# Restormer block, float32, one core: weight set-up behind the first LayerNorm, two more bands of depthwise convolution on TensorE, and a new issue order

## The chip, the cores and the metric

The kernel runs on one core of one Trainium2 chip. A core has five engines with a queue of instructions each: TensorE (PE: matmuls and transposes into PSUM), VectorE (DVE), ScalarE (ACT), GpSimd (POOL) and SyncE (SP); 16 DMA engines move data between the core's memory (SBUF) and HBM, or within SBUF. An engine takes its instructions in the order in which the program issued them, and waits on semaphores for the others. The metric is the device time of one execution in microseconds, the median of several runs. Everything is float32.

## What is computed

One transformer block on x of shape (16, 128, 96, 96): channel attention, then a feed-forward network with a depthwise 3x3 convolution. Cut to what matters:

```python
B, C, H, W = (16, 128, 96, 96); HEADS = 8; HID = 4 * C
x_hwc = x.transpose(0, 2, 3, 1)
xn1 = _layernorm(x_hwc, ln1_w, ln1_b)                  # LN1, over the 128 channels of each pixel
# attention over channels: q, k, v = xn1 @ w.T, q and k normalised over all 9216 pixels of an image,
# 16x16 attention per head, then @ wp.T
x = x + attn_out.transpose(0, 3, 1, 2)
xn2 = _layernorm(x_hwc, ln2_w, ln2_b).transpose(0, 3, 1, 2)   # LN2
h1 = jnp.einsum('bchw,oc->bohw', xn2, w_in[:, :, 0, 0])       # 128 -> 512 channels
h2 = lax.conv_general_dilated(h1, w_dw, ..., feature_group_count=HID)   # depthwise 3x3
h3 = jax.nn.gelu(h2, approximate=False)
x = x + jnp.einsum('bchw,oc->bohw', h3, w_out[:, :, 0, 0])    # 512 -> 128 channels
```

The kernel never forms q, k and v: it accumulates the Gram matrix of LN1's output over an image on TensorE, works out attention as one 128x128 matrix from it, and applies that matrix to the normalised pixels. So an image's attention can be worked out only when LN1 of the whole image is done.

## The kernel before

An image is cut into 8 bands of 12 rows (128 bands in all, numbered g), a band into 3 units of 4 rows, the 512 hidden channels into 4 chunks of 128. For a chunk of a band the depthwise convolution is done in one of two ways. In the usual way TensorE makes the hidden rows (`hidden`), ScalarE copies them out of PSUM (`kept`) and makes three or four of the nine products with a tap's weight, GpSimd issues DMAs that add two or three of these up and into the sum, VectorE does the other taps, and ScalarE applies gelu. For chunk 3 of some bands, TensorE does the convolution itself: nine matmuls of a unit with `comp`, the product of the tap's weight and w_in, accumulate in one PSUM bank; there is no hidden tensor, and gelu reads PSUM. `by_pe` says which bands:

```python
PE_CHUNK = 3
PE_BANDS = (0, 2, 4, 6, 8, 10)
PE_OF = 11
...
    def by_pe(g):
        return (NG - 1 - g) % PE_OF in PE_BANDS
    ...
        jobs += [(g, n) for n in range(NCH) if n != PE_CHUNK or not by_pe(g)]
```

The usual way, cut:

```python
    last = j == len(jobs) - 1
    third = n == THIRD_CHUNK and g % THIRD_OF in THIRD
    dma_taps = () if last else DMA_TAPS[: 3 if third else 2]
    left = [t for t in range(1, 9) if t not in dma_taps]
    for k, (r, e) in enumerate(chunks):                 # three pieces of a band's rows
        pe(..., at("hidden", jk), lambda r=r, e=e: hidden(r, e), ...)
        act(..., at("kept", jk), lambda r=r, e=e: kept(r, e), ...)
    act(..., at("product", j), lambda: product(0), h1, h3)
    for k, t in enumerate(dma_taps):
        act(..., at("products", jk), lambda t=t: product(t), h1, [("pr", (jn, t))])
    for k, t in enumerate(dma_taps[1:]):
        add(at("add_last", j), lambda t=t: add_products(t), ...)      # DMA, accumulating
    for k, t in enumerate(left):
        dve(..., at("tap", j + STEP["tap"] * k), lambda t=t: tap(t), h1, h3, True)
    if dma_taps:
        add(at("add_first", j), lambda: add_products(DMA_TAPS[0]), [pr[0]], h3)
    ...
        act(..., at("gelu", j), lambda s=s, e=e: gelu(s, e), [], h3[s:e])
```

The order in which instructions are issued is worked out on the host, before the launch, by a small plan. Every operation is entered with its engine, an assumed duration, what it reads and writes, a place (`at(kind, place)`: a position in the sequence of jobs plus a number per kind from the table `AT`), and the time after which its result is assumed to be there. The plan steps through time: an idle engine takes, of the operations whose inputs it takes to be ready and which find a buffer, the one with the lowest place. The order so found is the program; the chip keeps it, whatever the real times are.

```python
    def at(kind, place):
        return place + AT[kind]
```

The set-up of the weights is entered first. One operation on ScalarE's queue issues five weight loads; then TensorE transposes wq, wk and wp, then w_in, w_out and the nine tap products, four blocks to a PSUM bank, and VectorE copies each bank out:

```python
    op("ACT", 400, at("load_a", p), loads, [], mine, 900 + SLACK, dma=2 * T_MOVE)
    dve(400, at("weights", p), shifts, [], [("w", "in"), ("w", "conv"), ("w", "shift")])
    transposed(lambda: [v["wqk"][:, :P], v["wqk"][:, P:], v["wp"]], keep_qkp, ["qk"])
    ...
    transposed(lambda: [v["win"][:, n, :] for n in range(NCH)], ..., ["in"])       # winT
    transposed(lambda: [v["wout"][:, n * P : (n + 1) * P] for n in range(NCH)], ..., ["out"])
    for t0 in (0, 4, 8):                                                            # comp
        ...
```

LN1 and LN2 take 18 batches of four tiles of 128 pixels an image: TensorE transposes them (`forth`), VectorE takes statistics (BATCH_NORM_STATS2), GpSimd does the power -1/2, ScalarE (and for image 0 VectorE too) scales them into `zT`, TensorE adds zT to the Gram matrix (LN1) and transposes back (`back`), and ScalarE copies the result out (`place`).

Of the kernel before, what the change touches and what calls it, by code (L numbers as in the profile page):

```python
# [19 lines left out]
PE_CHUNK = 3  # L20
PE_BANDS = (0, 2, 4, 6, 8, 10)
PE_OF = 11
TINY = 1e-20
DMA_TAPS = (1, 2, 3)
THIRD, THIRD_OF, THIRD_CHUNK = (0,), 2, 1
# [3 lines left out]
X1_BUFS, XB_BUFS, PR_BUFS, H3_BUFS, ZT_BUFS = 2, 6, 5, 10, 3  # L29
IN_TURN = ("tr", "h3", "pr", "xb", "x1")  # L30
AT = dict(
    weights=13.95, zeros=3.15, load_a=-16.5, forth_a=-13.65, stats_a=-3.7, variance_a=-8.5, power_a=2.25,
    shift_a=-7.7, scaled_a=-1.8, gram=-2.7, back_a=-20.15, place_a=-18.95, attention=-16.9, mix=-10.45,
    residual=-13.95, mixed=-8.95, add_x=12.85, forth_b=-11.4, stats_b=-5.65, variance_b=-8.6,
    power_b=-18.6, shift_b=-25.05, scaled_b=-1.65, back_b=-21.6, place_b=-2.25, halo=2.3, hidden=-0.85,
    kept=-5.15, product=-7.7, products=3.3, add_last=-8.75, tap=4.45, add_first=25.8, gelu=-10.75,
    conv=0.1, conv_gelu=-5.7, out=3.25, add=-0.45, store=1.1,
)
STEP = dict(scaled=0.3, hidden=0.1, products=0.5, tap=0.166, conv=1.6, conv_tap=0.03, out=0.8, out_part=0.05)
SLACK = 300  # L40
NORM1_END = 6.0
EARLY = 5
WAIT = dict(POOL=350, SP=1300, ACT=1300)
T_POWER = 1000
T_ADD, T_MOVE = 3100, 1800


class Plan:
# [14 lines left out]
    def op(self, engine, ns, place, work, reads, writes, result, own=None, dma=0, two=False):  # L63

        k = len(self.ops)
        needs = {}  # L70
        for t in reads:
            if t in self.writer:
                needs[self.writer[t]] = True
        for t in writes:
            if t in self.writer:
                needs[self.writer[t]] = True
            for r in self.readers.get(t, ()):
                needs[r] = True
        for t in reads:
            self.readers.setdefault(t, []).append(k)  # L80
        new = []
        for t in writes:
            self.writer[t], self.readers[t] = k, []
            if t[0] in self.free and t[:2] not in self.users and t[:2] not in new:
                new.append(t[:2])
        for t in {t[:2]: None for t in (*reads, *writes)}:
            if t[0] in self.free:
                self.users.setdefault(t, []).append(k)
                needs[self.users[t][0]] = True
        needs.pop(k, None)  # L90
        self.ops.append((engine, ns, place, work, list(needs), new, result, own or result, dma, two))

    def order(self):
# [38 lines left out]
        def dispatch(engine, time):  # L132
# [19 lines left out]
            if o[8]:  # L152
                self.dma = max(time + ns + WAIT[engine], self.dma) + o[8]
                result = own = self.dma + result - time
# [48 lines left out]
def tile_restormer_block(  # L203
# [28 lines left out]
    NB, NU, UPB = H // BR, H // UR, BR // UR  # L232
# [101 lines left out]
    op = plan.op  # L334

    def at(kind, place):
        return place + AT[kind]

    def bank(key, n=4 * P):

        return banks[plan.slot["h", key]][:, :n]
# [18 lines left out]
    def pe(ns, p, f, r, w):  # L360
        op("PE", ns, p, f, r, w, ns + 200 + SLACK, ns)

    def dve(ns, p, f, r, w, two=False):
        op("DVE", ns, p, f, r, w, ns + 120 + SLACK, ns + 120, two=two)
# [29 lines left out]
    def weights(p):  # L394

        mine = [("h3", ("weights", k)) for k in range(2)]
        v, names = staged, iter(range(99))

        def loads():
            a, b = (h3p.tile([P, BR * W], F32, tag="h3", name=f"weights_{k}") for k in range(2))  # L400
            v["win"] = a[:, :HID].rearrange("p (n c) -> p n c", c=P)
            v["wout"], v["wp"] = a[:, HID : 2 * HID], a[:, 2 * HID : 2 * HID + P]
            v["wqk"], v["wqkT"] = b[:, : 2 * P], b[:, 2 * P : 4 * P]
            v["wt"] = b[:, 4 * P : 8 * P].rearrange("p (t c) -> p t c", c=P)
            nc.scalar.dma_start(out=v["wqk"][:, :P], in_=wq)
            nc.scalar.dma_start(out=v["wqk"][:, P:], in_=wk)
            nc.scalar.dma_start(out=v["wp"], in_=wp)
            nc.scalar.dma_start(out=v["win"], in_=w_in.rearrange("(n p) c kh kw -> p n (c kh kw)", p=P))
            nc.scalar.dma_start(out=v["wout"], in_=w_out.rearrange("c j kh kw -> c (j kh kw)"))

        def transposed(parts, kept, gives):

            key = ("weights", next(names))
            h = ("h", key)
            d = {}

            def forth():
                d["pt"] = bank(key)
                for k, part in enumerate(parts()):
                    nc.tensor.transpose(d["pt"][:, k * P : (k + 1) * P], part, ident)  # L420

            pe(440, at("weights", p), forth, mine, [h])
            dve(700, at("weights", p), lambda: kept(d["pt"]), [h], [("w", g) for g in gives] + mine[1:])

        def keep_qkp(pt):
            nc.vector.tensor_copy(v["wqkT"], pt[:, : 2 * P])
            nc.vector.tensor_scalar(wqkT, pt[:, : 2 * P], w1, None, ALU.mult)
            nc.vector.tensor_copy(wpT, pt[:, 2 * P : 3 * P])

        def biases():  # L430
            v["pc"] = bank(("weights", "biases"))[:1, : 2 * P]
            nc.tensor.matmul(v["pc"], lhsT=b1, rhs=v["wqkT"], start=True, stop=True)

        def comp_parts(ts):
            for t in ts:
                nc.vector.tensor_scalar(
                    v["wt"][:, t % 4, :], v["win"][:, PE_CHUNK, :], dw[:, PE_CHUNK, t : t + 1], None, ALU.mult
                )

        def shifts():  # L440

            nc.vector.tensor_tensor(none, w2, w2, ALU.mult)
            nc.vector.tensor_scalar(none, none, TINY * TINY, TINY, ALU.is_lt, ALU.mult)
            nc.vector.tensor_add(w2, w2, none)
            nc.vector.reciprocal(none, w2)
            nc.vector.tensor_mul(b2, b2, none)

        op("ACT", 400, at("load_a", p), loads, [], mine, 900 + SLACK, dma=2 * T_MOVE)
        dve(400, at("weights", p), shifts, [], [("w", "in"), ("w", "conv"), ("w", "shift")])
        transposed(  # L450
            lambda: [v["wqk"][:, :P], v["wqk"][:, P:], v["wp"]], keep_qkp, ["qk"]
        )
        pe(440, at("weights", p), biases, [("w", "qk"), mine[1]], [("h", ("weights", "biases"))])
        dve(400, at("weights", p), lambda: nc.vector.tensor_copy(cqk, v["pc"]), [("h", ("weights", "biases"))], [("w", "qk")])
        transposed(
            lambda: [v["win"][:, n, :] for n in range(NCH)],
            lambda pt: nc.vector.tensor_scalar(winT.rearrange("p n c -> p (n c)"), pt, w2, None, ALU.mult), ["in"],
        )
        transposed(
            lambda: [v["wout"][:, n * P : (n + 1) * P] for n in range(NCH)],  # L460
            lambda pt: nc.vector.tensor_copy(woutT.rearrange("p n c -> p (n c)"), pt), ["out"],
        )
        for t0 in (0, 4, 8):
            ts = range(t0, min(t0 + 4, 9))
            dve(170 * len(ts), at("weights", p), lambda ts=ts: comp_parts(ts), [mine[0]], [mine[1]])
            transposed(
                lambda ts=ts: [v["wt"][:, t % 4, :] for t in ts],
                lambda pt, ts=ts: nc.vector.tensor_scalar(
                    comp[:, ts[0] : ts[-1] + 1, :].rearrange("p t c -> p (t c)"), pt[:, : len(ts) * P],
                    w2, None, ALU.mult,  # L470
                ), ["conv"],
            )
# [18 lines left out]
    def norm(i, second, place_of):  # L491
# [41 lines left out]
        def pixels(s, m):  # L533
# [75 lines left out]
            dve(80, at("variance" + ab, s), variance, [], [bt])  # L609
            op("POOL", T_POWER, at("power" + ab, s), power, [], [bt], T_POWER + 33 + SLACK)  # L610
            dve(80, at("shift" + ab, s), shift, [], [bt])
# [320 lines left out]
            move(at("store", p), lambda: store(0, UPB), [("xb", (i, b), k) for k in range(UPB)], [], T_MOVE)  # L932

    def by_pe(g):
        return (NG - 1 - g) % PE_OF in PE_BANDS

    NG = B * NB
    jobs, first = [], []
    for g in range(NG):
        first.append(len(jobs))  # L940
        jobs += [(g, n) for n in range(NCH) if n != PE_CHUNK or not by_pe(g)]
# [3 lines left out]
    def job_of(g):  # L945

        return g * band

    weights(-17.0)
    zeros(-17.0)  # L950
    for i in range(B):
# [44 lines left out]
```

## Time and profile before

| | before |
|---|---|
| time, median of 3 runs | 4349.23 us (4347.39 to 4353.22) |
| span of the profiled execution | 4350.3 us |
| VectorE: taps of the convolution (L838) | 2590 x 1408 ns |
| TensorE: convolution matmuls (L889) | 3780 records, two to a float32 matmul |
| ScalarE: products (L834) | 946 x 1389 ns and 442 x 1366 ns |
| first tap on VectorE starts at | 103.02 us |

A profile is one execution of the program. In the table of engines each has its busy time, its share of the span, and the number of its instructions. In a row of stretches of time the same stands for a piece of the span, with the granted clock of TensorE and the share of the DMA engines. In the order of time a row gives the start, the length, the engine, the line of the kernel, the operation, and in brackets how long the engine was idle before it and what released it. A "q" behind an engine's name is its queue issuing a DMA; PEld is TensorE loading weights, which overlaps its matmuls.

### The profile page before, as it was taken

The page shows a single profiled execution, that of the slowest core. Times are in us where ns is not written, and L with a number is a line of the kernel's source. Part 1 is how long each engine was busy: PE and PEld are TensorE (multiplying, and loading weights), DVE is VectorE, ACT ScalarE, POOL GpSimd, SP SyncE. Part 2 cuts the span into 40 slices and gives each one's busy share as a digit, 9 for nine tenths or more (in the row PEclk, how much of TensorE's full clock was granted, in tenths as well). Part 3 has the DMA queues.
Part 4 walks back from the last instruction along what each step waited for, and adds up shares of the span by engine and source line. Part 5 has one row for each costly group of instructions (what it writes and reads, how often), then busy time and mean ns, then how long its engine had stood idle before and what let it go on. Part 6 is the DMA issues. An engine that isn't in the chain of part 4 may idle for free. (4 is left out here: it accounts for less than half of the span.)

```text
span 4350.3 us, 53308 instructions
## 1 busy us (share of the span) xinstructions
PE 4261.9 (98%) x17638; PEld 2717.5 (62%) x17638; DVE 4212.9 (97%) x5638; ACT 4136.9 (95%) x7240; POOL 1964.4 (45%) x1725
## 2 busy tenths in 40 slices
PE   7999999999999999999999999999999999999998
PEld 6666666666666666666666666666666666666554
DVE  6999999999999999999999999999999999999999
ACT  4999999999999999999999999999999999999996
POOL 3444544444444444444445444444444444454331
PEclk9999999999999999999999999999999999999999
DMA  2788898988998889888898988988889898898997
GB/s 79 161 183 190 170 202 179 186 189 174 192 192 186 183 173 193 180 189 180 180 190 188 190 178 176 192 189 181 183 184 191 174 200 178 179 196 160 190 185 156
DMA packets 193572, 785.23 MB, mean 180 GB/s; under 512 B 22416, under 2 KB 23824, under 8 KB 193296
## 3 DMA queue, kind: packets, MB, share of 16 engines
q0 software_dynamic: 153792, 630.00, 76.7%
q1 hardware_dynamic: 37152, 151.01, 9.6%
q8 instruction: 140, 2.29, 0.2%
q10 hardware_dynamic: 2352, 0.81, 0.1%
q14 instruction: 136, 1.11, 0.1%
HBM read 148.26 MB, written 75.50 MB: 51 GB/s over the span
## 5 line engine op out<-in xcount | busy, mean ns | idle before, releaser
L838 DVE SCALAR_TENSOR_TENSOR h<-h,dw,h 128x1152 f32<-128x1152 f32 x2590 | 3588.1, 1408 | 10.1 <-ACT h L834 6.9
L889 PE MATMUL h<-xn,comp 128*128 128x384 f32 x3780 | 1365.1, 486 | 2.2 <-ACT h L823 2.2
L834 ACT ACTIVATE pr<-h,dw 128x1152 f32<-128x1152 f32 x946 | 1290.5, 1389 | 3.9 <-DMA pr<-pr 3.6
L912 PE MATMUL h<-h,woutT 128*128 128x384 f32 x3072 | 1149.2, 489 | 13.2 <-ACT h L823 4.8
L818 PE MATMUL h<-xn,winT 128*128 128x384 f32 (+1 forms) x2652 | 1051.6, 503 | 25.1 <-ACT h L823 14.2
L889 PEld LDWEIGHTS h<-xn,comp 128*128 128x128 f32 x3780 | 689.7, 189 | 431.4 <-issue 9.2
L842 POOL DMA_DIRECT2D pr<-pr x505 | 461.9, 915 | 823.0 <-ACT pr L834 656.5
L823 ACT COPY h<-h 128x384 f32<-128x384 f32 (+1 forms) x1326 | 727.6, 607 | 61.6 <-PE h L818 49.2
L912 PEld LDWEIGHTS h<-h,woutT 128*128 128x128 f32 x3072 | 557.7, 190 | 355.8 <-issue 16.9
L842 POOL DMA_DIRECT2D h<-pr x441 | 425.0, 964 | 701.9 <-PE h L818 98.8
L818 PEld LDWEIGHTS h<-xn,winT 128*128 128x128 f32 x2652 | 472.3, 190 | 331.4 <-issue 47.9
L567 POOL TENSOR_TENSOR rstd_a<-ve_a,mhalf 128x4 f32<-128x4 f32 x288 | 517.3, 1799 | 326.8 <-DVE ve_a L563 311.6
L567 POOL TENSOR_TENSOR rstd_b<-ve_b,mhalf 128x4 f32<-128x4 f32 x288 | 526.9, 1830 | 295.1 <-DVE ve_b L563 276.6
L846 ACT ACTIVATE h<-h 128x1152 f32<-128x1152 f32 (+1 forms) x444 | 561.4, 1265 | 50.6 <-DMA h<-pr 48.5
L834 ACT ACTIVATE h<-h,dw 128x1152 f32<-128x1152 f32 x442 | 603.3, 1366 | 5.4 <-PE h L912 3.3
L588 ACT ACTIVATE zT<-pT_b,nb_b,rstd_b 128x128 f32<-128x128 f32 x1132 | 459.1, 580 | 1.4 <-DVE nb_b L571 0.7
L588 ACT ACTIVATE zT<-pT_a,nb_a,rstd_a 128x128 f32<-128x128 f32 x1080 | 442.9, 601 | 4.0 <-DVE nb_a L571 3.9
L598 PEld LDWEIGHTS g<-zT 128*128 128x128 f32 x2304 | 297.4, 192 | 57.6 <-issue 5.6
L598 PE MATMUL g<-zT 128*128 128x129 f32 x2304 | 305.5, 275 | 0.0
L507 PE MATMUL h<-xn,mwT 128*128 128x384 f32 x768 | 288.0, 488 | 3.1 <-ACT h L823 1.0
L632 ACT ACTIVATE xn<-pB_b,b 128x384 f32<-128x384 f32 x384 | 270.6, 705 | 8.8 <-PE pB_b L628 8.8
L634 ACT COPY xn<-pB_a 128x384 f32<-128x384 f32 x384 | 237.2, 618 | 23.9 <-PE pB_a L628 23.7
(145 smaller groups left out, 3371.4 us busy)
## 6 DMA issues: line engine op xcount, KB each, us to landing
pr<-pr POOLq DMA_DIRECT2D x505, 576.0 KB, 6.1
h<-pr POOLq DMA_DIRECT2D x441, 576.0 KB, 6.8
x<-in_x_dram SPq DMA_DIRECT2D x128, 576.0 KB, 6.4
out_dram<-x SPq DMA_DIRECT2D x127, 576.0 KB, 5.4
x<-in_x_dram POOLq DMA_DIRECT2D x122, 576.0 KB, 7.3
out_dram<-x SPq DMA_DIRECT2D x3, 192.0 KB, 1.9
weights<-in_L_conv_w_in_dram ACTq DMA_DIRECT2D x1, 256.0 KB, 10.8
weights<-in_L_conv_w_out_dram ACTq DMA_DIRECT2D x1, 256.0 KB, 11.7
```

Source lines behind the costliest of these rows:

```text
L507: nc.tensor.matmul(rows(pm), lhsT=mats[i][0], rhs=interior(i, u), start=True, stop=True)
L567: nc.gpsimd.tensor_tensor(rstd, d["ve"], mhalf, ALU.pow)
L588: nc.scalar.activation(zT(q)[:, k, :P], d["pT", q][:, k, :], AF.Identity, bias=d["nb"][:, t : t + 1], scale=d["rstd"][:, t : t + 1],)
L598: nc.tensor.matmul(grams[i][:, : P + 1], lhsT=zt[:, :P], rhs=zt, start=(q == 0 and k == 0), stop=(q == NU * TPU // QT - 1 and k == QT - 1),)
L818: nc.tensor.matmul(rows(ph), lhsT=winT[:, n, :], rhs=window(xn, r0 + r, e - r, 1), start=True, stop=True)
L823: nc.scalar.copy(window(h1_, r, e - r, 1), rows(d.pop(("ph", r))))
L834: nc.scalar.activation(to, shifted(t), AF.Copy, scale=dw[:, n, t : t + 1])
L838: nc.vector.scalar_tensor_tensor(h3, shifted(t), dw[:, n, t : t + 1], h3, ALU.mult, ALU.add)
L842: nc.gpsimd.dma_start(out=to, in_=d["pr", t], accum_op=ALU.add)
L846: nc.scalar.activation(h3, h3, AF.Gelu)
L889: nc.tensor.matmul(d["pc"], lhsT=comp[:, t, :], rhs=window(xn, r0 + dy, UR, dx), start=(t == 0), stop=(t == 8),)
L912: nc.tensor.matmul(rows(d["po"]), lhsT=woutT[:, n, :], rhs=h3s[g, n][:, s * UR : (s + 1) * UR, :], start=(k == 0), stop=(k == NCH - 1),)
```

## The change

Three things are changed, all in the plan that fixes the order. First, the plan takes the weights as loaded only after 20 us instead of 1.2 us beyond their transfer, so that the set-up's transposes are ordered behind LN1's first batches: TensorE is not to stand before a weight that has not landed while image data have. Second, in the last image six of the eight bands have chunk 3 convolved by TensorE, where the old rule gave four: the last image has no LN1 of a next image beside it. Counted from the end these are bands 0, 1, 2, 4, 5 and 7 instead of 0, 2, 4 and 6; all other images keep the old rule. Third, the numbers of the table `AT` are new, so that every queue has a new order. Buffers, instructions and the rest of the arithmetic are the same.

```diff
+PE_LAST = (0, 1, 2, 4, 5, 7)
...
 AT = dict(
-    weights=13.95, zeros=3.15, load_a=-16.5, forth_a=-13.65, stats_a=-3.7, variance_a=-8.5, power_a=2.25,
-    shift_a=-7.7, scaled_a=-1.8, gram=-2.7, back_a=-20.15, place_a=-18.95, attention=-16.9, mix=-10.45,
-    residual=-13.95, mixed=-8.95, add_x=12.85, forth_b=-11.4, stats_b=-5.65, variance_b=-8.6,
-    power_b=-18.6, shift_b=-25.05, scaled_b=-1.65, back_b=-21.6, place_b=-2.25, halo=2.3, hidden=-0.85,
-    kept=-5.15, product=-7.7, products=3.3, add_last=-8.75, tap=4.45, add_first=25.8, gelu=-10.75,
-    conv=0.1, conv_gelu=-5.7, out=3.25, add=-0.45, store=1.1,
+    weights=10.45, zeros=-0.55, load_a=-15.15, forth_a=-12.6, stats_a=-5.05, variance_a=-7.4,
+    power_a=-1.65, shift_a=-5.8, scaled_a=-2.25, gram=-2.15, back_a=-19.55, place_a=-30,
+    attention=-11.35, mix=-10.3, residual=-15.8, mixed=-15.6, add_x=2.25, forth_b=-11.95, stats_b=-3.7,
+    variance_b=-5.4, power_b=-20.6, shift_b=-22.65, scaled_b=-2.4, back_b=-19.15, place_b=-0.55,
+    halo=4.55, hidden=-1.65, kept=-8.9, product=-7.6, products=2.05, add_last=-4.65, tap=7.3,
+    add_first=25.4, gelu=-4.85, conv=-0.8, conv_gelu=-6.2, out=2.3, add=7.1, store=-8.95,
 )
...
+T_WEIGHTS = 20000
...
-        op("ACT", 400, at("load_a", p), loads, [], mine, 900 + SLACK, dma=2 * T_MOVE)
+        op("ACT", 400, at("load_a", p), loads, [], mine, T_WEIGHTS, dma=2 * T_MOVE)
...
     def by_pe(g):
-        return (NG - 1 - g) % PE_OF in PE_BANDS
+        k = NG - 1 - g
+        return k in PE_LAST if k < NB else k % PE_OF in PE_BANDS
```

## Prediction, before the changed kernel was run

> **What bounds the kernel now.** I read the table of engines first, then the middle and the end of the span by stretches of time, and last the opening in order of time. The first says only that four engines are nearly full:
>
> ```profile
> PE 4261.9 (98%) x17638; PEld 2717.5 (62%) x17638; DVE 4212.9 (97%) x5638; ACT 4136.9 (95%) x7240; POOL 1964.4 (45%) x1725
> ```
>
> The stretches show where the few idle microseconds lie (columns: stretch, its length, then busy us and instructions of PE, PEld, DVE, ACT, POOL; granted clock, DMA share, GB/s):
>
> ```profile
> 0.00:25.00 25.00, 9.12 (x34) 6.22 (x35) 7.70 (x30) 3.16 (x6) 6.16 (x26) 0.86 0.66 221
> 25.00:50.00 25.00, 23.61 (x194) 22.66 (x194) 19.96 (x76) 15.54 (x39) 12.71 (x26) 0.94 0.01 2
> 50.00:75.00 25.00, 20.30 (x130) 16.77 (x129) 14.66 (x52) 10.48 (x27) 4.66 (x5) 0.81 0.19 50
> ...
> 1000.00:2000.00 1000.00, 991.10 (x4109) 630.92 (x4108) 974.66 (x1297) 970.92 (x1705) 468.22 (x397) 1.00 0.89 185
> ...
> 4050.00:4250.00 200.00, 190.27 (x653) 111.78 (x652) 198.06 (x217) 188.17 (x303) 76.08 (x71) 0.99 0.93 187
> 4250.00:4300.00 50.00, 42.36 (x121) 23.91 (x120) 48.45 (x41) 38.21 (x51) 11.29 (x13) 0.90 0.77 160
> 4300.00:4351.00 51.00, 40.32 (x118) 22.39 (x116) 44.96 (x39) 20.70 (x28) 6.90 (x8) 0.95 0.66 145
> ```
>
> Three regimes. In the middle VectorE is busy 974.7 of 1000 us, ScalarE 970.9, and TensorE is level with them. TensorE's busy figure counts overlapping matmuls, so I rate it by throughput instead: in the chain of waits, ten records of 384 columns take 3.23 us, so 0.323 us each (a float32 matmul of the program is two records), a 480-column one by scaling 0.404; sixteen 128-column Gram records took 1.95 us, 0.112 each after the first. Between 1000 and 2000 us the groups list 2304 records of 384 columns, 104 of 480 and 1593 of 128, plus some tens of small ones: 744 + 42 + 178 + about 15 = 979 us. So three engines are within 1% of each other and the middle has no single bound. In the last 300 us VectorE alone is full (291.5 of 301 us) and ScalarE and TensorE loosen. In the first 75 us every engine is idle part of the time, so a latency chain rules there:
>
> ```profile
> 8.37 0.45 PE L420 MATMUL h<-ident,weights 128*128 128x128 f32 x1 [8.37 <-DMA weights<-in_L_conv_wq_dram]
> ...
> 11.43 0.48 PE L420 MATMUL h<-ident,weights 128*128 128x128 f32 x1 [1.94 <-DMA weights<-in_L_conv_wp_dram]
> ...
> 11.69 1.92 PE L549 MATMUL h<-ident,x 128*128 128x128 f32 x8
> ...
> 18.54 1.09 PE L420 MATMUL h<-ident,weights 128*128 128x128 f32 x4 [3.99 <-DMA weights<-in_L_conv_w_in_dram]
> 19.67 0.75 DVE L457 TENSOR_SCALAR winT<-h,w 128x512 f32<-128x512 f32 x1 [4.47 <-PE h L420]
> ...
> 20.87 0.71 DVE L580 TENSOR_SCALAR zT<-h,st_a,rstd_a 128x128 f32<-128x128 f32 x2
> ...
> 58.88 0.29 DVE L694 COPY gs<-g 128x129 f32<-128x129 f32 x1 [0.75 <-PE g L598]
> ```
>
> The reader is to see that TensorE waits for three small weights up to 11.43 us and again 3.99 us for w_in, while image data are there already: the first image transpose at 11.69 has no wait of its own. The first normalised tile is made only at 20.87 us; the Gram sum of image 0, which attention needs, is copied at 58.88 us; the first convolution tap of VectorE starts at 103.02 us.
>
> **What the skill says.** PSUM — Partial Sum Buffer, Engine vs sequencer instructions, states that the queues of ScalarE, VectorE and GpSimd are strict FIFO and that matmuls start in program order. The trace agrees: the image's transpose stands still behind a weight's. TensorE: Matmul & The Clock Gate, What's actually happening, says that an idle window of about 3.4 us drops the array to half clock; here, after the 3.99 us wait, the granted clock was 0.50 from 18 to 27 us. Perfetto Trace Analysis, Identifying the Most-Contended Engine, warns that matmul busy time is no measure of TensorE's headroom; hence my throughput count.
>
> **Part 1, setup behind LN1.** Nothing is removed. In the order of the changed kernel TensorE begins with the transposes of x bands 0 and 1, and the first weight transpose stands only after LN1 batch 17's transposes; the weight loads are issued in the same place as before. VectorE still begins with the five small operations on the LN2 weights, which waited for a load until 7.20 us and end at 8.13 us. x band 0 is issued at 0.81 us and the nine x loads took 3.9 us at the least to land, 5.6 in the median, so it is there by about 6.5. So the first statistics come at about 8.2 us where they came at 12.87; then as before some 1.1 us of statistics, 0.15, one power of 1.01 us and 0.15 with their hand-overs, so that the first scaling comes at about 11.5 us instead of 20.87: 9.4 us earlier. From there to the Gram copy took 38.0 us for 18 batches. I keep that: in both orders eight setup matmuls stand inside this stretch (0.15 us each: four took 0.60), and the half-clock stretch only moves. Behind the Gram the new order has 13 setup matmuls where the old had 5, which I put at 1 us. All bands of x had landed by 18.9 us (the DMA share falls to zero), so bands do not run short. Attention and the run-up to the first tap keep their order nearly (182 rows of VectorE before the first tap, 186 before), so the first tap should start at about 94 us (103.02 - 9.4 + 1), 9 us earlier. It lies on the path: behind it all three engines are full. **-9 us.**
>
> **Part 2, two more bands on TensorE.** The old rule took bands 0, 2, 4, 6 from the end; the new takes 0, 1, 2, 4, 5, 7. For each of the two net bands:
> - VectorE loses 6 taps of 1.41 us: 8.5 us. Both: 16.9 us.
> - TensorE gains 27 matmuls, 54 records x 0.323 = 17.4 us, and loses three hidden matmuls, 4 x 0.404 + 2 x 0.323 = 2.3 us. Net 15.2 us. Both: 30.4 us.
> - ScalarE loses 3 products of 1.29, 3 copies (1.7 us together) and a gelu of 1.20, and gains 3 gelus of about 0.55: 5.1 us. Both: 10 us. Two accumulating DMAs a band go too.
>
> From 4050 us on TensorE's throughput time is 730 x 0.323 + 30 x 0.404 + 130 x 0.112 = 262.5 us of 301. It becomes 292.9; VectorE's 291.5 becomes 274.6. So the bound of the tail passes from VectorE at 291.5 to TensorE at 292.9: the two bands overshoot the balance, and an honest sum gives about 0. What speaks for a small gain is the drain: before, TensorE was idle at the end while VectorE finished, and the new order puts all of the last three bands' chunk 3 on TensorE, ahead of the last taps. I choose **-3 us** between -10 and +5.
>
> **Part 3, the new order.** Some 37 priorities change and every queue is reshuffled; the work and the 32 table loads of ScalarE are the same. Idle in the middle is about 2.5% of VectorE, 2% of TensorE: 100 us in all, of which a re-tuning on the same structure might win or lose a tenth. The order was presumably chosen for a lower end, so **-4 us**, between -16 and +12. No row of the profile fixes this; it is the loosest term.
>
> Sum: 4349 - 9 - 3 - 4 = 4333 us.
>
> **Rivals.** (a) The start is hidden: LN1 starts earlier, but attention 0 waits for the weights now transposed behind it, or the first bands wait for winT and comp. For it: wqkT, cqk, winT and comp stand between LN1 batch 17 and the attention steps in the new order, and comp's nine parts pass through VectorE in turn. Against: 13 matmuls, five evacuations of 0.3 to 0.75 us and comp's nine products of 0.27 us are some 8 us spread over two engines that were busy only 14.66 and 20.30 of 25 us between 50 and 75 us. That rival would leave 2 to 5 us of the 9: about 4338. (b) VectorE's relief counts in full: the tail shortens by 16.9 us and the time is about 4320. For it: VectorE never rests from 4050 to 4343 us. Against: TensorE's 292.9 us above. (c) TensorE becomes the bound and, with its queue in order, matmuls of the last bands hold back the output products, so the tail grows by 5 to 10 us: about 4344. (d) The new order is worse on the chip than planned, a wait on a buffer repeated in all 16 images; 1 us an image would be +16: about 4353.
>
> **Range and chances.** Start -5 to -11, tail -10 to +5, middle -16 to +12. The middle dominates; I take the terms as independent and get some 16 us to each side in most cases, a little wider on account of the middle: 4308 to 4354. Two per cent is 87 us; no term or sum of terms gets near it on either side, so within 2% is nearly certain.
>
> **What would show it.** In the profile after: first statistics near 8 us, Gram copy near 50, first tap near 94 (if it is past 99, rival a). From 4050 us on, busy VectorE falls below TensorE's throughput count, and ScalarE loosens; if the last taps end at the same distance from the end as before with VectorE still full, rival b. The middle: VectorE's busy share per 1000 us against 974.66; each 1% of it is about 40 us of the time. The prediction is wrong if that share moves by more than 0.4%, which no count of instructions would have told.

## Result and profile after

The changed kernel takes 4333.42 us (median of 6 runs, 4330.35 to 4339.06) beside 4349.4 us for the kernel before: ratio 0.9964, 95% interval 0.9951 to 0.9977. That is 16 us less, 10 to 21 by the interval.

The table of engines and stretches of the span (columns as before):

```profile
PE 4279.2 (99%) x17734; PEld 2732.2 (63%) x17734; DVE 4196.3 (97%) x5626; ACT 4125.7 (95%) x7232; POOL 1935.5 (45%) x1721
```

```profile
0.00:25.00 25.00, 15.12 (x93) 13.92 (x94) 13.07 (x53) 7.97 (x18) 9.85 (x25) 1.00 0.66 222
25.00:50.00 25.00, 23.42 (x204) 22.10 (x203) 20.28 (x74) 16.18 (x40) 11.97 (x15) 1.00 0.08 25
50.00:75.00 25.00, 19.79 (x109) 15.59 (x108) 12.91 (x46) 9.21 (x24) 4.52 (x24) 0.80 0.25 72
...
1000.00:2000.00 1000.00, 993.32 (x4117) 633.66 (x4116) 979.36 (x1303) 974.27 (x1709) 461.70 (x400) 1.00 0.89 186
2000.00:3000.00 1000.00, 988.90 (x4113) 630.46 (x4111) 970.39 (x1295) 969.58 (x1707) 460.07 (x397) 1.00 0.88 183
...
4250.00:4300.00 50.00, 50.00 (x157) 29.32 (x156) 49.89 (x41) 36.11 (x47) 11.20 (x13) 1.00 0.86 172
4300.00:4334.00 34.00, 29.78 (x93) 17.23 (x91) 19.36 (x19) 7.53 (x12) 0.86 (x1) 0.98 0.34 92
```

Three things are to be seen. The first 25 us hold 13.07 us of VectorE work, against 7.70 before. The middle has no trend: VectorE's busy time rises in one 1000 us and falls in the next. Near the end TensorE is full (50.00 of 50 us; it had 42.36 between 4250 and 4300 us).

The opening in order of time:

```profile
5.50 3.65 PE L551 MATMUL h<-ident,x 128*128 128x128 f32 x16 [5.50 <-DMA x<-in_x_dram]
...
7.25 0.16 DVE L444 TENSOR_TENSOR none<-w 128x1 f32<-128x1 f32 x1 [6.19 <-DMA w<-in_L_conv_ln_w_dram]
...
8.11 1.42 DVE L558 BATCH_NORM_STATS2 st_a<-h 128x6 f32<-128x256 f32 x4
...
11.17 0.73 DVE L582 TENSOR_SCALAR zT<-h,st_a,rstd_a 128x128 f32<-128x128 f32 x2
...
50.42 0.29 DVE L696 COPY gs<-g 128x129 f32<-128x129 f32 x1
...
95.76 1.42 DVE L840 SCALAR_TENSOR_TENSOR h<-h,dw,h 128x1152 f32<-128x1152 f32 x1 [1.32 <-ACT h L836]
```

TensorE now starts on image data at 5.50 us, and no weight stands before them. The first scaling is 9.7 us earlier than before, the Gram copy 8.5 us, the first tap 7.3 us.

The groups of TensorE's matmuls in the last 300 us, and the end in order of time:

```profile
L891 PE MATMUL h<-xn,comp 128*128 128x384 f32 x378 | 133.2, 486 | 0.0
L914 PE MATMUL h<-h,woutT 128*128 128x384 f32 x271 | 99.3, 487 | 0.0
L820 PE MATMUL h<-xn,winT 128*128 128x384 f32 x156 | 58.2, 486 | 0.0
L509 PE MATMUL h<-xn,mwT 128*128 128x384 f32 x36 | 13.1, 486 | 0.0
```

```profile
4313.16 5.77 DVE L840 SCALAR_TENSOR_TENSOR h<-h,dw,h 128x1152 f32<-128x1152 f32 x4
4316.72 13.06 PE L914 MATMUL h<-h,woutT 128*128 128x384 f32 x40
4329.82 0.56 DVE L921 TENSOR_TENSOR x<-h,x 128x384 f32<-128x384 f32 x1 [2.02 <-PE h L914]
```

In the kernel before, the groups with the longest idle time ahead of them (last column) in its last 300 us were these two:

```profile
L912 PE MATMUL h<-h,woutT 128*128 128x384 f32 x264 | 98.8, 501 | 7.9 <-ACT h L846 4.4 <-DVE x L919 2.5 <-ACT h L823 1.1
L818 PE MATMUL h<-xn,winT 128*128 128x384 f32 x160 | 63.5, 502 | 10.8 <-ACT h L823 10.2 <-ACT x L516 0.6
```

TensorE now waits for nothing in its last 300 us. Its throughput count, made as in the prediction, is 841 x 0.323 + 24 x 0.404 + 130 x 0.112 = 296 us of 300, where it was 262.5 of 301. VectorE's last tap ends at 4318.9 us, 14.4 us before the end of the span, where in the kernel before it ended 6.6 us before the end. From 4316.72 us TensorE makes 40 records of output product back to back, for 13.06 us; a last addition and the store follow.

**A finer ruler.** Shares of busy time do not say where 16 us went, so I set milestones: the start of VectorE's first tap, and the start of the 192nd output-product record of each image (the group has 3072, 192 an image). Against the profile of before, the changed kernel is 7.3 us ahead at the first tap, 10.4 at image 0's milestone, 11.9 at image 12's, 17.0 at the end of the span. So most of it is there when image 0 is done, the middle gave nothing to speak of in this execution, the last three images 5 us. A milestone is read from one execution, and executions of one program differ by some microseconds: the times below decide, the milestones only say where.

### The profile page after: what moved, and what is told of

It is laid out like the page before. It is cut to its first block, busy times and chain, and to the rows that moved or that the text cites. A ratio compares the mean times of both kernels' runs of the same rounds, so it can differ in the third digit from the quotient of the medians.

```text
span 4333.3 us, 53606 instructions
## 1 busy us (share of the span) xinstructions
PE 4279.2 (99%) x17734; PEld 2732.2 (63%) x17734; DVE 4196.3 (97%) x5626; ACT 4125.7 (95%) x7232; POOL 1935.5 (45%) x1721
## 4 chain that ended last, share of the span: by engine, by line
PE 40%; DVE 21%; ACT 15%; DMA 5%; issue 4%; POOL 2%; POOLq 0%; DVEq 0%; ACTq 0%
DVE h L840 17%; PE h L891 13%; PE h L914 9%; PE h L820 8%; ACT pr L836 4%; ACT zT L590 3%; DMA h<-pr 3%; ACT h L825 2%; PE g L600 2%; PE h L509 2%; ACT h L836 2%; ACT h L848 2%; DMA pr<-pr 1%; PE pT_b L551 1%; PE pB_b L630 1%
## 5 line engine op out<-in xcount | busy, mean ns | idle before, releaser
L891 PE MATMUL h<-xn,comp 128*128 128x384 f32 x3888 | 1409.4, 487 | 1.4 <-DVE x L921 0.9
L891 PEld LDWEIGHTS h<-xn,comp 128*128 128x128 f32 x3888 | 705.6, 190 | 424.4 <-issue 10.0
L844 POOL DMA_DIRECT2D h<-pr x439 | 413.1, 941 | 780.6 <-DVE h L840 129.2
L569 POOL TENSOR_TENSOR rstd_a<-ve_a,mhalf 128x4 f32<-128x4 f32 x288 | 504.6, 1758 | 370.3 <-DVE ve_a L565 340.3
```

The source lines that it names most:

```text
L569: nc.gpsimd.tensor_tensor(rstd, d["ve"], mhalf, ALU.pow)
L844: nc.gpsimd.dma_start(out=to, in_=d["pr", t], accum_op=ALU.add)
L891: nc.tensor.matmul(d["pc"], lhsT=comp[:, t, :], rhs=window(xn, r0 + dy, UR, dx), start=(t == 0), stop=(t == 8),)
```

## The experiments

All times are ratios to the kernel before on the same chip, whose median was 4349.4 us beside the changed kernel and 4350.04 (e1 to e4), 4354.36 (e5 to e8) and 4355.07 us (e9 to e12) in the three sets. 0.001 is 4.35 us.

| kernel | ratio (95%) | against before, us | start to first tap | first tap to image 0 | image 0 to 12 | image 12 to end |
|---|---|---|---|---|---|---|
| changed | 0.9964 (0.9951 to 0.9977) | -16 | -7.3 | -3.2 | -1.5 | -5.1 |
| e1 weights only | 0.9987 (0.9981 to 0.9994) | -6 | -6.5 | -1.3 | -0.9 | +1.0 |
| e2 bands only | 1.0035 (1.0022 to 1.0047) | +15 | +0.6 | +4.0 | +7.1 | +3.3 |
| e3 order only | 1.0014 (1.0006 to 1.0022) | +6 | +0.8 | -0.4 | -2.5 | +5.3 |
| e4 changed, old bands | 1.0000 (0.9992 to 1.0009) | 0 | -7.7 | -0.5 | -1.5 | +4.1 |
| e5 bands, spacing held | 1.0003 (0.9997 to 1.0010) | +1 | -0.7 | -0.5 | +6.4 | +3.1 |
| e6 spacing alone | 1.0044 (1.0032 to 1.0057) | +19 | +0.4 | +3.5 | +19.4 | +2.0 |
| e7 changed, spacing held | 0.9991 (0.9983 to 0.9999) | -4 | -7.2 | -0.2 | +6.5 | +4.1 |
| e8 changed, old bands, new spacing | 0.9970 (0.9959 to 0.9982) | -13 | -7.2 | -3.0 | -4.0 | +1.7 |
| e9 changed, again | 0.9957 (0.9944 to 0.9971) | -19 | -7.5 | -3.2 | +0.5 | -3.0 |
| e10 changed, constant lead | 0.9963 (0.9950 to 0.9975) | -16 | -7.2 | -0.4 | -6.1 | 0.0 |
| e11 changed, more drift | 0.9984 (0.9978 to 0.9991) | -7 | -6.1 | +3.8 | +5.8 | -8.2 |
| e12 changed, five bands | 0.9978 (0.9970 to 0.9986) | -10 | -7.3 | -1.8 | -1.7 | +4.5 |

The last four columns are milestones against the one profile of before. Between sets they carry the chip and the one execution too: in e5 all engines have the same order as before until the last image, and it still reads +6.4 in the middle. So a difference of some 6 us in the column of the middle says nothing by itself.

### Each part alone

**e1, the weights.** On the kernel before:

```diff
+T_WEIGHTS = 20000
...
-        op("ACT", 400, at("load_a", p), loads, [], mine, 900 + SLACK, dma=2 * T_MOVE)
+        op("ACT", 400, at("load_a", p), loads, [], mine, T_WEIGHTS, dma=2 * T_MOVE)
```

> The kernel before with the plan's time for the weight loads set to 20 us alone; old bands, old table of places. Theory 1 (the gain of the start is the set-up standing before image data): Gram copy of image 0 near 50 us, first tap near 95, the lead of 8 to 9 us lasts to the end: about 4341 us. Theory 2 (the new order gives the gain of the start): first tap near 101 to 103 and 4347 to 4350 us.

Measured 0.9987. In its order of time on VectorE:

```profile
11.23 0.72 DVE L581 TENSOR_SCALAR zT<-h,st_a,rstd_a 128x128 f32<-128x128 f32 x2
...
51.65 0.28 DVE L695 COPY gs<-g 128x129 f32<-128x129 f32 x1
96.56 4.33 DVE L839 SCALAR_TENSOR_TENSOR h<-h,dw,h 128x1152 f32<-128x1152 f32 x3 [0.33 <-ACT h L835]
```

The start is that of the changed kernel with the old table, and the lead of 6.5 us is still there at the end of the span (7.7 us). Theory 1 stands in its mechanism, a little smaller: 6 us, 3 to 8 by the interval.

**e2, the bands.** On the kernel before, `PE_LAST` and the new `by_pe`, nothing else.

> The kernel before with six bands of the last image on TensorE alone. Theory 1 (the tail's gain comes from moving two bands): the trace starts and runs as before to 4000 us and the tail is 7 us shorter: about 4342 us. Theory 2 (the sum of the prediction: TensorE becomes the bound, nothing is gained unless the order suits it): 4347 to 4352 us. Two jobs fewer also shift where the normalisations are placed against the convolutions in all images, so the middle may move by some us.

Measured 1.0035: 15 us slower, which neither theory has, though the last sentence of the expectation names the way. The loss grows from image 0 on (11.7 us by image 12), while the bands differ only in image 15. What else the edit moves is in these lines of the kernel:

```python
    band = len(jobs) / NG
    def job_of(g):
        return g * band
```

A job is one chunk of one band that is convolved in the usual way. Normalisations and attention are placed at `job_of`, convolutions at the true number of their job. With 442 jobs in 128 bands the two keep step (the first 120 bands hold 414 jobs, 3.45 a band, and the spacing is 3.453). Two jobs fewer make the spacing 3.4375: the normalisations run ahead of the convolutions by 0.0156 job a band, 1.9 jobs by image 15, one job in the mean.

**e3, the table.** On the kernel before, the new `AT` alone.

> The kernel before with the new table of places alone; old weight time, old bands. Theory 1 (the order is worth nothing in the middle, as the milestones of the two traces say): start as before, 4347 to 4352 us. Theory 2 (the prediction's third term): about 4345 us. Theory 3 (the order carries the tail's gain): about 4342 us.

Measured 1.0014, 6 us slower, which none of the three theories has: the new table alone is worth less than nothing.

**e4, all but the bands.** On the changed kernel:

```diff
-        return k in PE_LAST if k < NB else k % PE_OF in PE_BANDS
+        return k % PE_OF in PE_BANDS
```

> The changed kernel with the old rule for the bands: four of the last image's eight on TensorE. Theory 1 (the two bands carry the tail): the lead at the end of the start, 8 to 9 us, is all that is left: about 4341 us, with VectorE full to the last taps. Theory 2 (the new order carries the tail): about 4334 us.

Measured 1.0000: neither theory. In the profiled execution the start's lead is there (7.7 us) and 4 us of it go after image 12; the median of its runs, 4351.46 us, lies another 5 us above that execution (4346.38). But this edit too puts the spacing back to 442/128. So weights and table without the new spacing give nothing that can be measured; that is also the sum of e1 (-6) and e3 (+6).

### Bands and spacing apart

**e5, bands without spacing.** On the kernel before, `PE_LAST` as in the change, and:

```diff
-    band = len(jobs) / NG
+    band = (len(jobs) + 2) / NG
```

> The kernel before with six bands of the last image on TensorE, the mean spacing of a band in jobs, by which the normalisations are placed, held at its old 442/128. Theory 1 (the 15 us that the bands-only kernel lost by image 13 came from the spacing, 440/128, and not from the bands, which only exist in the last image): the milestones of images 0 to 13 lie within 3 us of before; the end 0 to 7 us earlier: 4343 to 4350 us. Theory 2 (the loss came from elsewhere): about 4365 us with the same drift.

**e6, spacing without bands.** On the kernel before:

```diff
-    band = len(jobs) / NG
+    band = (len(jobs) - 2) / NG
```

> The kernel before with the old bands and only the spacing changed from 442/128 to 440/128. Theory 1 (spacing costs the middle): images 0 to 13 drift to about 12 to 15 us late, 4360 to 4366 us. Theory 2: as before, 4347 to 4352 us.

**e7, the changed kernel without spacing**: the diff of e5 on the changed kernel.

> The changed kernel with the spacing held at 442/128. Theory 1 (the new table of places is there to suit the new spacing, and wins back what the spacing loses): with the old spacing the middle is no better than in the changed kernel, within 4 us, and the last image's normalisations come later: 4333 to 4342 us. Theory 2 (spacing costs under any table): the middle gains some 10 us: about 4324 us.

**e8, the changed kernel with spacing, without bands**: the diffs of e4 and e6 on the changed kernel.

> The changed kernel with the old four bands, spacing kept at 440/128 as in the change, so that it differs from the changed kernel in the two bands alone. Theory 1 (the two bands shorten the tail by 7 to 18 us under the new order): start and middle as in the changed kernel to image 13, then the end later by that: 4341 to 4351 us. Theory 2 (the spacing, by placing the last image's normalisations earlier, gives the tail's gain): about 4335 us.

Measured 1.0003, 1.0044, 0.9991, 0.9970. Spacing alone costs 19 us under the old table (e6), theory 1 and more than the 12 to 15 it had; the bands without the new spacing cost nothing (e5), theory 1 again, though nothing is gained at the end. So e2's loss is the spacing's. Under the new table it gains: 13 us from e4 to e8, 12 to 15 from e7 to the changed kernel. So e7's theory 2 falls, and theory 1 is right only in direction: the new table does suit the new spacing, but with the old one the kernel takes 4351.06 us, 4 under before on its chip, where the range I gave meant 7 to 16. And e8's theory 1 falls: without the two bands, but with the spacing, 13 of the 16 us are there. Theory 2 has the amount, but by the milestones the gain does not lie in the tail, where it had put it. The bands are worth little everywhere: +1 us on the kernel before (e5), -4 from e4 to e7, -3 to -6 from e8 to the two measurements of the changed kernel. In each of these comparisons the intervals overlap, so a gain of the bands is not shown.

How much work the engines got through between 300 and 3700 us shows the spacing's effect on one chip. One line each for e5, e6 (old table) and e7, e8 (new table), old spacing first:

```profile
300.00:3700.00 3400.00, 3362.17 (x13997) 2147.29 (x13996) 3316.72 (x4402) 3297.64 (x5802) 1586.04 (x1350) 1.00 0.89 184
```

```profile
300.00:3700.00 3400.00, 3354.20 (x13950) 2142.53 (x13949) 3305.57 (x4390) 3285.36 (x5782) 1606.38 (x1347) 1.00 0.88 184
```

```profile
300.00:3700.00 3400.00, 3368.22 (x13991) 2140.45 (x13990) 3315.55 (x4404) 3298.58 (x5802) 1565.23 (x1350) 1.00 0.88 184
```

```profile
300.00:3700.00 3400.00, 3372.88 (x14074) 2152.07 (x14073) 3324.18 (x4422) 3313.02 (x5833) 1572.84 (x1358) 1.00 0.89 185
```

Under the old table the new spacing leaves 47 of TensorE's records and 12 of VectorE's instructions undone in that time; under the new one it gets 83 and 18 more done. All of PE, DVE and ACT move the same way, by 5 to 15 us of busy time. No single wait carries it: between e5 and e6 VectorE's wait for the power of LN1 in the middle goes from 22.3 to 28.3 us, ScalarE's gelu for its accumulating DMA from 30.5 to 37.9; between e7 and e8 the gelu's wait goes from 26.3 to 17.8, ScalarE's copy of hidden rows from 38.9 to 26.2.

### What the new order's lead is, and how far it goes

**e9**: the changed kernel beside the next three.

> The changed kernel as it stands, run beside the next three on their chip: 0.9964 of before, that is 14 to 18 us under it.

**e10, a constant lead for a growing one.** On e7:

```diff
-        return g * band
+        return g * band - 1
```

> The changed kernel with the old spacing of 442/128, so that nothing drifts, and instead all normalisations placed one job earlier, which is the mean over the images of what the new spacing does. Theory 1 (what counts is how far ahead of the convolutions the normalisations stand on average): as the changed kernel, within 4 us. Theory 2 (no such law: an order is good or bad by its details, and the table was found for this one order): nearer to the kernel with the spacing held and no lead, 3 to 8 us under before.

**e11, twice the drift.** On the changed kernel, the diff of e6 (438/128).

> The changed kernel with the spacing lowered once more by the same step, 438/128. Theory 1 (with this table an earlier place is better, and 440 is on the way): another 5 to 12 us under the changed kernel. Theory 2 (the table was found for 440, any other spacing loses): 5 to 20 us over the changed kernel.

**e12, five bands.** On the changed kernel, spacing kept at 440/128:

```diff
-PE_LAST = (0, 1, 2, 4, 5, 7)
+PE_LAST = (0, 1, 2, 4, 7)
...
-    band = len(jobs) / NG
+    band = (len(jobs) + 1 - 2) / NG
```

> The changed kernel with five bands of the last image on TensorE (0, 1, 2, 4, 7 from the end) in place of six, spacing held at 440/128. By the count of the prediction TensorE's throughput time in the last 300 us is 15 us lower than with six and VectorE's 8 us higher, 278 against 283, the best balance: theory 1 (the count rules the tail): 4 to 9 us under the changed kernel. Theory 2 (the tail is ruled by its order and its last waits): within 4 us of the changed kernel or slower.

Measured 0.9957, 0.9963, 0.9984, 0.9978. The changed kernel again is 19 us under before, 1 us more than expected. One job of constant lead takes as long as the drift (e10): theory 1 there. Twice the drift loses 12 of the 19 us (e11): theory 2. Under this table a mean lead of 0, 1 and 2 jobs gives 0.9991, 0.9957 and 0.9984, so one job is the best of the three; under the old table a drift with a mean of one costs 19 us. So the best of these settings depends on the table; which of its numbers makes the difference was not tried and stays open.

That the lead as such is the cause is not shown. Between the first tap and image 0's milestone, where the drift is still small (0.0156 job a band, 8 bands an image), the new spacing already loses 4.0 and 3.5 us under the old table (e2, e6) and gains 3.2, 3.0, 3.2 and 1.8 under the new one (changed, e8, e9, e12), while twice the drift loses 3.8 (e11). And e10, with a whole job of lead there, gains only 0.4 in that stretch. The rival stays open: that any shift regroups the instructions, and that which grouping wins has no law as simple as a lead.

Five bands lose 9 us to six, where the count had said a gain of 4 to 9 (e12): theory 2. The changed kernel and e12 between 4050 and 4250 us:

```profile
4050.00:4250.00 200.00, 200.00 (x694) 119.99 (x693) 198.85 (x209) 184.78 (x295) 70.30 (x69) 1.00 0.91 183
```

```profile
4050.00:4250.00 200.00, 189.27 (x635) 110.73 (x634) 197.64 (x209) 184.83 (x292) 70.11 (x69) 0.97 0.91 184
```

TensorE is full in the first and not in the second; VectorE is nearly full in both. Groups of e12 in its last 300 us, the last column the idle time ahead of them:

```profile
L914 PE MATMUL h<-h,woutT 128*128 128x384 f32 x256 | 94.2, 496 | 4.2 <-ACT h L825 3.4 <-DVE x L921 0.7
L820 PE MATMUL h<-xn,winT 128*128 128x384 f32 x154 | 58.8, 495 | 3.9 <-ACT h L825 2.3 <-ACT h L897 0.6 <-ACT x L518 0.6
```

TensorE there waits 14 us in all, mostly for ScalarE's copies, and in the changed kernel not at all. But VectorE can carry the loss as well. In both kernels its last tap ends 14.4 us before the end of the span, with the same 40 records of output product around and behind it, and in the 285.6 us up to that tap it is busy 282.0 us (changed) and 279.8 us (e12). The six taps that e12 has more take 8.5 us, which is nearly the whole loss. The count had left out what follows the last tap: 283 + 14 us for five bands is no better than TensorE's 293 for six. No run separates these two accounts. What is shown is that the count, as it was made, did not set the tail; nor are five bands faster than four with the same spacing (e8, 0.9970).

No other version beats the changed kernel; the intervals of e8 and e10 overlap with its own.

## Why the prediction was right, and where it was not

The time is right: 4333.0 predicted, 4333.42 measured. The terms are not all: -9, -3 and -4 were forecast; e1, e8 and the changed kernel give about -6 for the start, -7 for the order (e8 less e1: -13 + 6), -3 to -6 for the bands. The errors cancelled, so the agreement to 0.4 us is luck. That each part was in its range (-11 to -5, -16 to +12, -10 to +5) is what the prediction can claim.

**Part 1, the start: mechanism right, size too large.** The sum itself was rounded up: -9.4 + 1 is -8.4, not -9. First statistics were forecast at 8.2 us (8.11), the first scaling at 11.5 (11.17), the Gram copy near 50 (50.42), the first tap at 94 (95.76). What was short is the 38.0 us that I kept from first scaling to Gram copy: it was 39.3, and why is open (nine set-up matmuls stand in it where I counted eight, far too little for 1.3 us). The 1 us for the setup behind the Gram was nearly right: the stretch to the first tap grew from 44.1 to 45.3. The lead of 6.5 us at the first tap reached the end in e1, so rival (a), a hidden start, falls.

**Part 2, the bands: the bound right, the gain not shown.** TensorE became the bound of the tail, at 296 us of throughput where I had 292.9, though VectorE too is nearly full up to its last tap. The relief of VectorE did not count in full (rival b): the two bands bring 3 to 6 us by the ratios, and nothing on the old order (e5). The -3 is neither confirmed nor refuted, since the intervals overlap. My reason for a small gain was a shorter drain: chunk 3 of the last bands ahead of the last taps. The last convolution matmul does end before the last tap (at 4316.9 us, the tap at 4318.9), but the drain behind that tap grew from 6.6 us to 14.4. In the kernel before, its last tap was

```profile
4342.26 1.41 DVE L838 SCALAR_TENSOR_TENSOR h<-h,dw,h 128x1152 f32<-128x1152 f32 x1
```

Now 33 records of output product stand behind the last tap, where eight did. That is rival (c) in kind, output products held back; but the tail as a whole did not grow by 5 to 10 us, it is 5 and 3 us shorter in the two profiles.

**Part 3, the order: the step that failed.** I took the new order for the numbers of the table (39, not some 37) and gave it -4, on the presumption that it was chosen for a lower end. The table alone costs 6 us. What I overlooked is that the bands enter the number of jobs, that number the spacing, and the spacing the place of every normalisation in all 16 images. Spacing alone costs 19 us, table alone 6, both together gain 7 on top of the weights. Rival (d), a worse order in all 16 images, is what e6 shows; in the change it does not occur: this table with this spacing is 13 us faster than with the old one (e4 to e8). Why the two go together stays open.

**What would show it.** I had written that the prediction is wrong if VectorE's share in the middle moves by more than 0.4%. It moved by +0.5% and -0.6% in neighbouring 1000 us, so by this sign it was wrong, but the sign was of no use: the milestones from image 0 to 12 moved by 1.5 us only. Milestones of equal work showed what shares did not.

## What to carry to other kernels

When an order is computed by a plan, look for every quantity that an edit feeds into the plan: here a rule for the last image moved the place of work in all images, which cost more than the edit itself could win. A table of priorities that suits one setting need not suit the next: here the effect of the same shift turned sign with the table. So try parts with the rest held, and count equal work, not busy shares. A throughput count per engine gives the lowest time of a stage, if what must follow an engine's last work is added to it; whether an order reaches it has to be measured.

## What the runs showed of the hardware that I had not expected

At the start of the changed kernel TensorE ran at half its later pace without the clock column saying so. There, with 1.00 shown between 10 and 20 us, eight Gram records took 1.93 us at 15.06 us, and thirteen took 1.62 us at 18.66:

```profile
15.06 1.93 PE L600 MATMUL g<-zT 128*128 128x129 f32 x8
...
18.66 1.62 PE L600 MATMUL g<-zT 128*128 128x129 f32 x13
```

In the kernel before, eight Gram records took the same time in a stretch (24 to 27 us) for which the column says 0.50, and full pace came only at about 28 us (five in 0.78 us at 27.97):

```profile
24.75 1.93 PE L598 MATMUL g<-zT 128*128 128x129 f32 x8
```

So the slow stretch moved forward with the start, as the prediction assumed; the column alone would have said that it vanished.
